# Merging eight expert matrices after a gate: a half block by TensorE, one wide chain on VectorE, and tile 5 of the last norm on GpSimd

## The chip, the cores and the metric

The kernel runs on one core of a Trainium2 chip (trn2). The metric is the device time of one execution in microseconds (us); the median of several runs is compared. Engines are called as in the profile: PE (TensorE), PEld (its weight loads), DVE (VectorE), ACT (ScalarE), POOL (GpSimd) and SP (the queue that issues the DMAs).

## The reference

One layer of a graph network on 1250 nodes of 512 features: a graph convolution (two rounds), a linear attention, and at the end a feed-forward block whose weights are merged by a gate. Only the last part is touched:

```python
gh = relu(x @ gfc1_w.T + gfc1_b)
g = (gh @ gfc2_w.T + gfc2_b).mean(over nodes)       # 8 numbers, one for each expert
W1m = W1 + sum_e g[e] * tv_W1[e]                    # 256 x 512
b1m = b1 + g @ tv_b1
W2m = W2 + sum_e g[e] * tv_W2[e]                    # 512 x 256
b2m = b2 + g @ tv_b2
h = relu(x @ W1m.T + b1m)
res = x + h @ W2m.T + b2m
out = x_before + layernorm(res) * lng + lnb
```

Here `x` is the normalised input of the block. Nothing of the merged weights can be computed before the gate is known, and the gate needs a sum over all nodes.

## The kernel before, in words

Nodes are tiled by 128 (`NT` = 10 tiles, the last of 98 rows), features by 128 (`DT` = 4 chunks), the hidden size 256 is `FT` = 2 halves. The layer runs in stages; from `last_order` on, the order of instructions on every engine is the order of the program text, so a line that stands earlier is also queued earlier on its engine, and an engine works through its own queue strictly in that order.

After the gate products (L1278, L1281) `gate` (L1297, DVE) holds the eight numbers on every partition, and `gate9` (L1298, ACT) holds them as columns. The merged first weight `m1` has four chunks `c` of 128 x 256, the merged second weight `m2` has two halves of 128 x 512. Each is a sum of nine terms. Two helpers make such sums:

- `merge` (L1309): ACT writes the first scaled term into a PSUM bank (`scaled`, L1307), DVE adds seven scaled terms one after the other (L1312), and a last addition (L1315) adds the unscaled weight. With `alone=True` DVE does all of it.
- `merge_far` (L1317): ACT scales each of the eight terms in place, POOL adds each to the weight (L1320).

Chunk 0 of `m1` is made by DVE alone, chunks 1 and 2 by `merge`, chunk 3 by ACT and POOL (L1347), the first half of `m2` by `merge` and the second by `merge_far`. `joined(c)` (L1322) multiplies chunk `c` with the transposed input into six PSUM banks, `parts`: two halves of the hidden size by three column blocks of 418, 416 and 416 nodes. After chunk 3 ACT applies the ReLU (L1328) and writes `a_t`. The vector `b2` (the merged bias) is one product (L1334), copied by ACT (L1342), and is added to the input `xn2` tile by tile: tiles 0 to 4 by DVE (L1364), 5 to 9 by POOL (L1366). PSUM has eight banks: six `parts` and two `sums`.

The last loop makes each tile `t` of the output: `out_product` (L1374, two products of 512 columns), `out_sum` (adds `xn2`), `out_gauge` (mean and variance), and then one of two endings. `out_far` normalises on ACT and does two additions or products of 512 on POOL. `out_near` does three instructions on DVE (L1413 to L1416). For the tiles in `BY_SCALAR` ACT computes the variance (L1398) instead of DVE. These lists and the delay of the near tiles stand in two places:

```python
NEAR, BY_SCALAR = (4, 5, 7, 8, 9), (5, 7, 8, 9)
for t in range(NT + 3):
    for u in NEAR:
        if u == t - (3 if u in BY_SCALAR else 1):
            out_near(u)
```

Each tile's store is issued on SP, in the order of the tiles.

Of the kernel before, what the change touches and what calls it, by code (L numbers as in the profile page):

```python
# [9 lines left out]
F32 = mybir.dt.float32  # L10
# [31 lines left out]
CHUNKS = [(0, 418), (418, 416), (834, 416)]  # L42


def rows(t):
    return min(P, N - t * P)
# [479 lines left out]
def usual_block(  # L526
# [23 lines left out]
    nc = tc.nc  # L550
# [3 lines left out]
    tmp = ctx.enter_context(tc.tile_pool(name="tmp", bufs=2))  # L554
# [7 lines left out]
    def bank(dtype=F32):  # L562
        return psum.tile([P, 512], dtype, tag="bank", name="bank")
# [14 lines left out]
    ident = const.tile([P, P], F32, name="ident")  # L578
# [49 lines left out]
    def v(name, i=0, n=1):  # L628
        at = _COLS[name][0] + i
        return v_sb[:, at:at + n]  # L630
# [43 lines left out]
    g2bc = const.tile([NE, 1], F32, name="g2bc")  # L674
# [108 lines left out]
    key = e_d  # L783
# [352 lines left out]
    gate9 = late.tile([NE + 1, P], F32, name="gate9")  # L1136
# [137 lines left out]
    pg, pg9 = bank(), bank()  # L1274
# [20 lines left out]
    gate_products([DT - 1])  # L1295
    gate = late.tile([P, NE], F32, name="gate")
    nc.vector.scalar_tensor_tensor(gate, pg[:, 0:NE], 1.0 / N, v("g2b", 0, NE), op0=ALU.mult, op1=ALU.add)  # L1297
    nc.scalar.activation(gate9[0:NE, :], pg9[0:NE, 0:P], AF.Identity, bias=g2bc, scale=1.0 / N)  # L1298

    a_t = more.tile([P, FT, N], F32, tag="E", name="a_t")
    parts = [(f, b, bank()) for f in range(FT) for b in range(len(CHUNKS))]
    sums = [bank(), bank()]

    def scaled(dst, e, src):
        nc.scalar.activation(dst, src, AF.Copy, scale=gate[:, e:e + 1])  # L1307

    def merge(acc, dst, srcs, at, alone=False):  # L1309

        for e in range(0 if alone else 1, NE):
            nc.vector.scalar_tensor_tensor(dst[at] if alone and e == NE - 1 else acc, srcs[e][at], gate[:, e:e + 1],  # L1312
                                           dst[at] if alone and e == 0 else acc, op0=ALU.mult, op1=ALU.add)
        if not alone:
            nc.vector.tensor_tensor(dst[at], acc, dst[at], ALU.add)  # L1315

    def merge_far(dst, srcs, at):  # L1317
        for e in range(NE):
            scaled(srcs[e][at], e, srcs[e][at])
            nc.gpsimd.tensor_tensor(dst[at], dst[at], srcs[e][at], ALU.add)  # L1320

    def joined(c):  # L1322
        for f, b, ps in parts:
            c0, cn = CHUNKS[b]
            nc.tensor.matmul(ps[:, :cn], m1[:, c, f * P:(f + 1) * P], xn2_t[:, c, c0:c0 + cn],
                             start=(c == 0), stop=(c == DT - 1))
# [3 lines left out]
    def first(c):  # L1330
        return (slice(None), c, slice(None))


    nc.tensor.matmul(sums[1], gate9, r9[:, 0, :], start=True, stop=True)  # L1334
    b2 = late.tile([P, D], F32, name="b2")
# [24 lines left out]
    joined(3)  # L1360
    for t in range(NT):
        n = rows(t)
        if t < NT // 2:
            nc.vector.tensor_tensor(xn2[0:n, t, :], xn2[0:n, t, :], sums[0][:n], ALU.add)  # L1364
        else:
            nc.gpsimd.tensor_tensor(xn2[0:n, t, :], xn2[0:n, t, :], b2[:n], ALU.add)  # L1366

    last = {}

    def out_product(t):  # L1370
        n = rows(t)
        last[t] = bank()
        for f in range(FT):
            nc.tensor.matmul(last[t][:n], a_t[:, f, t * P:t * P + n], m2[:, f, :], start=(f == 0), stop=(f == FT - 1))  # L1374


    NEAR, BY_SCALAR = (4, 5, 7, 8, 9), (5, 7, 8, 9)

    def out_sum(t):
        n = rows(t)  # L1380
        ps = last[t]
        if t in BY_SCALAR:
            mv = small.tile([P, 2], F32, name="mv")
            nc.vector.scalar_tensor_tensor(ps[:n], ps[:n], 1.0, xn2[0:n, t, :], op0=ALU.mult, op1=ALU.add,
                                           accum_out=mv[:n, 0:1])
            last[t] = ps, mv
        else:
            nc.vector.tensor_tensor(ps[:n], ps[:n], xn2[0:n, t, :], ALU.add)

    def out_gauge(t):  # L1390

        n = rows(t)
        if t in BY_SCALAR:
            ps, mv = last[t]
            rs = small.tile([P, 2], F32, name="rs")
            m = out_row(t)
            nc.scalar.mul(mv[:n, 0:1], mv[:n, 0:1], -1.0 / D)
            nc.scalar.activation(m[:n], ps[:n], AF.Square, bias=mv[:n, 0:1], accum_out=mv[:n, 1:2])  # L1398
            nc.scalar.activation(rs[:n, 0:1], mv[:n, 1:2], AF.Sqrt, bias=eps[:n], scale=1.0 / D)
            last[t] = ps, mv, rs, m  # L1400
        else:
            last[t] = (last[t],) + spread(last[t][:n], n) + (None,)

    def out_row(t):
        tag, bufs = (("row", 3), ("xt", 4))[t % 2]
        return tmp.tile([P, D], F32, tag=tag, bufs=bufs, name="m")

    def out_near(t):

        n = rows(t)  # L1410
        ps, mv, rs, m = last[t]
        m = out_row(t) if m is None else m
        nc.vector.scalar_tensor_tensor(ps[:n], ps[:n], mv[:n, 0:1], ln_g[:n],  # L1413
                                       op0=ALU.add if t in BY_SCALAR else ALU.subtract, op1=ALU.mult)
        nc.vector.reciprocal(rs[:n, 0:1], rs[:n, 0:1])  # L1415
        nc.vector.scalar_tensor_tensor(m[:n], ps[:n], rs[:n, 0:1], x_sb[0:n, t, :], op0=ALU.mult, op1=ALU.add)  # L1416
        nc.sync.dma_start(out=out[t * P:t * P + n, :], in_=m[:n])

    def out_far(t):

        n = rows(t)
        ps, mv, rs, _ = last[t]
# [88 lines left out]
```

## Time and profile before

| what | value |
|---|---|
| median of 3 runs | 571.74 us (571.64 to 572.16) |
| the profiled execution | 570.89 us, its span 569.1 us |
| `gate` is written | at 517.2 us of the span |
| first product with `m1` (L1325) | at 521.5 us |
| first product with `m2` (L1374) | at 540.4 us |
| last product ends | at 557.7 us |
| last instruction of DVE ends | at 563.2 us |

The span is the time from the first to the last instruction in one execution with the profiler on; the time of that execution is longer by 1.8 us, and the median of the runs without a profile lies 0.85 us above that. A row of the profile names the line, the engine, the operation, the tiles (out<-in), the shape and the count; durations are of one instruction, and on a pipelined engine the distance from one start to the next can be shorter than the duration. A product of f32 operands appears as two records on PE.

### The profile page before, as it was taken

What the parts mean: (1) busy time and instruction counts of PE and PEld (TensorE: products, weight loads), DVE (VectorE), ACT (ScalarE), POOL (GpSimd) and SP (SyncE); (2) the same over time, 40 slices, a digit from 0 to 9 for tenths busy, and PEclk for the clock granted to TensorE, in tenths of its full rate; (3) what the DMA queues carried; (4) which work ended last, traced back from release to release, by engine and by line L of the source; (5) the groups of instructions that cost most, each with busy time, mean ns of one, the idle gap of its engine ahead of it and who ended that gap; (6) DMA issues with size and microseconds to landing.
All of it is one profiled execution on the core that took longest, in us unless ns stands there. A gap on an engine that the chain in (4) does not pass through costs nothing. (4 is left out here: it accounts for less than half of the span.)

```text
span 569.1 us, 6958 instructions
## 1 busy us (share of the span) xinstructions
PE 545.6 (96%) x2367; PEld 368.1 (65%) x2367; DVE 324.7 (57%) x1097; ACT 244.2 (43%) x539; POOL 75.3 (13%) x73
## 2 busy tenths in 40 slices
PE   8799999999999999999999999999999999997992
PEld 7655568799955567777754454449995556864540
DVE  4579999976899724444425534121112248726885
ACT  6676664554354212223333344112333446726453
POOL 8200000000000000000004331000000001204972
PEclk9999999999999999999999999999999999997997
DMA  9500200020021010000311102000008320402014
GB/s 282 184 1 1 74 2 1 1 75 2 1 94 56 0 75 0 1 1 2 104 44 37 37 1 74 0 0 1 2 0 282 124 74 1 147 1 75 0 41 146
DMA packets 19285, 29.10 MB, mean 51 GB/s; under 512 B 1529, under 2 KB 8185, under 8 KB 19240
## 3 DMA queue, kind: packets, MB, share of 16 engines
q1 hardware_dynamic: 19096, 28.52, 14.8%
q8 instruction: 20, 0.33, 0.2%
q14 instruction: 25, 0.20, 0.1%
q10 hardware_dynamic: 144, 0.05, 0.0%
HBM read 26.01 MB, written 2.56 MB: 50 GB/s over the span
## 5 line engine op out<-in xcount | busy, mean ns | idle before, releaser
L981 PE MATMUL bank<-adj,y_h 128*128 128x416 f32 (+1 forms) x240 | 86.5, 361 | 1.1 <-DVE adj L851 1.1
L834 DVE TENSOR_SCALAR oh_k<-count,e_d 128x240 f16<-128x240 f16 x324 | 84.4, 281 | 0.0
L981 PE MATMUL bank<-adj,y_l 128*128 128x416 f32 (+1 forms) x240 | 84.4, 352 | 0.0
L1083 POOL TENSOR_TENSOR m<-m,ls_bc 128x512 f32<-128x512 f32 (+1 forms) x10 | 12.7, 1270 | 447.6 <-ACT m L600 447.6
L968 PE MATMUL bank<-w,h_t 128*128 128x512 f32 (+1 forms) x160 | 70.4, 592 | 0.0
L576 PE MATMUL bank<-z_t,w 128*128 128x416 f32 (+1 forms) x192 | 68.9, 513 | 0.0
L576 PEld LDWEIGHTS bank<-z_t,w 128*128 128x128 f32 x192 | 36.1, 189 | 31.8 <-issue 30.0
L832 DVE TENSOR_SCALAR oh_s<-count,s_lo 128x128 f16<-128x128 f16 x220 | 55.8, 254 | 0.0
L968 PEld LDWEIGHTS bank<-w,h_t 128*128 128x128 f32 (+1 forms) x160 | 29.4, 188 | 34.8 <-issue 34.5
L614 DVE SCALAR_TENSOR_TENSOR z_t<-u,m_sb,z_t 128x416 f32<-128x416 f32 (+1 forms) x24 | 15.7, 652 | 59.8 <-ACT u L613 59.8
L981 PEld LDWEIGHTS bank<-adj,y_h 128*128 128x128 f32 x240 | 45.1, 188 | 2.6 <-issue 2.1
L981 PEld LDWEIGHTS bank<-adj,y_l 128*128 128x128 f32 x240 | 45.2, 188 | 1.2 <-issue 0.7
L849 PE MATMUL bank<-oh_k,oh_s 128*128 128x240 f16 x324 | 41.8, 266 | 1.6 <-ACT oh_s L818 1.2
L849 PEld LDWEIGHTS <-oh_s 128*128 128x128 f16 x324 | 31.6, 98 | 16.4 <-issue 5.3
L612 ACT ACTIVATE z_t<-bank,v_sb 128x416 f32<-128x416 f32 (+1 forms) x24 | 14.7, 610 | 61.4 <-PE bank L981 61.4
L851 DVE TENSOR_TENSOR adj<-adj,bank 128x240 f32 x81 | 32.7, 404 | 13.9 <-PE bank L849 12.5
L995 DVE BATCH_NORM_STATS2 bst<-bank 128x6 f32<-128x416 f32 (+1 forms) x24 | 14.4, 600 | 42.9 <-ACT h_t L994 42.9
L917 PE MATMUL bank<-kk,xn 128*128 128x128 f32 (+1 forms) x320 | 38.4, 275 | 0.0
L576 PE MATMUL bank<-xn_t,lw 128*128 128x256 f32 (+2 forms) x128 | 36.6, 428 | 0.8 <-ACT xn_t L607 0.8
L917 PEld LDWEIGHTS bank<-kk,xn 128*128 128x128 f32 (+1 forms) x320 | 37.0, 192 | 0.1
L1064 PE MATMUL bank<-mixer,q_t 128*128 128x512 f32 (+1 forms) x80 | 36.3, 592 | 0.0
L576 PE MATMUL bank<-xn_t,gw 128*128 128x256 f32 (+2 forms) x128 | 35.3, 427 | 0.9 <-ACT xn_t L607 0.9
(172 smaller groups left out, 797.3 us busy)
## 6 DMA issues: line engine op xcount, KB each, us to landing
t<-in_tv_w SPq DMA_DIRECT2D x12, 512.0 KB, 7.6
w<-in_conv_w SPq DMA_DIRECT2D x4, 1024.0 KB, 5.4
x_in<-in_x SPq DMA_DIRECT2D x9, 256.0 KB, 4.7
xt<-in_x SPq DMA_DIRECT2D x9, 256.0 KB, 4.2
out<-m SPq DMA_DIRECT2D x9, 256.0 KB, 2.7
rest<-in_tv_w SPq DMA_DIRECT2D x4, 512.0 KB, 5.1
lw<-in_lin_w SPq DMA_DIRECT2D x4, 256.0 KB, 5.1
wk<-in_w_qkv SPq DMA_DIRECT2D x1, 1024.0 KB, 7.1
```

The lines of the kernel that those rows point to most:

```text
L576: nc.tensor.matmul(ps[:, :cn], lhs(c), rhs(c), start=(c == 0), stop=(c == k - 1))
L612: nc.scalar.activation(dst, ps[:, :cn], AF.Relu, bias=v(*bias))
L614: nc.vector.scalar_tensor_tensor(dst, u[:, :cn], minus(*slope), dst, op0=ALU.mult, op1=ALU.add)
L832: nc.vector.tensor_scalar(oh_s[:, j, :], count16[:, 0:P], s_lo[:, b, j:j + 1], None, op0=ALU.is_equal)
L834: nc.vector.tensor_scalar(oh_k[:, j, :], count16, key[:, b, j:j + 1], None, op0=ALU.is_equal)
L849: nc.tensor.matmul(ps[:, 0:NT * W], oh_s[:, j, :], oh_k[:, j, :], start=(j == 0), stop=(j == J - 1))
L851: nc.vector.tensor_tensor(adj_r[:, :, at], adj[:, :, at], ps[:, 0:NT * W].rearrange("p (s d) -> p s d", s=NT), ALU.add)
L917: nc.tensor.matmul(ps[:, c * P:(c + 1) * P], xn[0:n, t, c * P:(c + 1) * P], k_nodes(f)[0:n, t, :], start=(t == 0), stop=(t == NT - 1))
L968: nc.tensor.matmul(ps[:n], h_t[:, c, t * P:t * P + n], w1[:, c, :], start=(c == 0), stop=(c == DT - 1))
L981: nc.tensor.matmul(ps[:, :cn], y[0:n, s, f * P:(f + 1) * P], adj_r[0:n, s, c0:c0 + cn], start=(s == 0 and y is ys[0]), stop=(s == NT - 1 a ...
L995: nc.vector.bn_stats(st[:, b, :], ps[:, :cn])
L1064: nc.tensor.matmul(ps[:n], q_t[:, h, t * P:t * P + n], mixer[:, h, :], start=(h == 0), stop=(h == DT - 1))
```

## The change

- The first 128 columns of chunk 0 of `m1` are summed by PE: a product of the identity with the unscaled weight, and eight products whose stationary operand is an identity scaled by `gate[e]` (`gated`, six made by DVE, two by ACT). ACT copies the sum from PSUM to `m1`. The other 128 columns are a chain of eight on DVE, as before but half as wide.
- Chunk 1 of `m1` is made by ACT and POOL. Chunks 2 and 3 are one chain on DVE of 512 columns.
- `gate9` is scaled later, and the product for `b2` and its copy move behind `joined(1)`. `b2` is copied once; tiles 0 to 5 of `xn2` are shifted by DVE from the PSUM bank, tiles 6 to 9 by POOL.
- The second half of `m2` is begun (two of eight terms) ahead of that copy, the rest follows it.
- The order of `parts` changes: by column block first. In `joined(3)` only the first four products come ahead of the output tiles; the last two, for the third column block, come ahead of tile 5.
- Tile 5 leaves `NEAR` and `BY_SCALAR`, so POOL ends six tiles and DVE four; the delay of the `BY_SCALAR` tiles is 2 in place of 3.

```diff
-    nc.scalar.activation(gate9[0:NE, :], pg9[0:NE, 0:P], AF.Identity, bias=g2bc, scale=1.0 / N)
...
-    parts = [(f, b, bank()) for f in range(FT) for b in range(len(CHUNKS))]
+    parts = [(f, b, bank()) for b in range(len(CHUNKS)) for f in range(FT)]
...
-    nc.tensor.matmul(sums[1], gate9, r9[:, 0, :], start=True, stop=True)
-    merge(sums[0][:, 0:FF], m1, t1s, first(0), alone=True)
...
-    scaled(t1s[0][first(3)], 0, t1s[0][first(3)])
-    nc.scalar.copy(b2, sums[1])
-    scaled(sums[1][:, 0:FF], 0, t1s[0][first(1)])
+    gated = [tmp.tile([P, 2, P], F32, tag="xt", bufs=4, name="gated") for _ in range(NE // 2)]
+    one = [flat(t, 1, 2) for t in t1s]
+    two = [flat(t, 2, 4) for t in t1s]
+    for e in (0, 1, 2, 4, 5, 6):
+        nc.vector.tensor_scalar(gated[e // 2][:, e % 2, :], ident, gate[:, e:e + 1], None, op0=ALU.mult)
+    scaled(gated[1][:, 1, :], 3, ident)
+    merge_far(flat(m1, 1, 2), one, [0])
+    scaled(gated[3][:, 1, :], 7, ident)
+    merge_far(flat(m1, 1, 2), one, [1, 2])
+    nc.tensor.matmul(sums[1][:, 0:P], ident, m1[:, 0, 0:P], start=True, stop=False)
     for e in range(NE):
-        if e:
-            scaled(t1s[e][first(3)], e, t1s[e][first(3)])
-        nc.gpsimd.tensor_tensor(m1[first(3)], m1[first(3)], t1s[e][first(3)], ALU.add)
-    joined(0)
-    scaled(sums[0][:, 0:FF], 0, t1s[0][first(2)])
-    merge(sums[1][:, 0:FF], m1, t1s, first(1))
-    joined(1)
-    merge_far(m2, t2s, first(1))
-    scaled(sums[1], 0, t2s[0][first(0)])
-    merge(sums[0][:, 0:FF], m1, t1s, first(2))
-    joined(2)
+        nc.tensor.matmul(sums[1][:, 0:P], gated[e // 2][:, e % 2, :], t1s[e][:, 0, 0:P],
+                         start=False, stop=(e == NE - 1))
+    acc = sums[0][:, 0:FF - P]
+    for e in range(NE):
+        nc.vector.scalar_tensor_tensor(m1[:, 0, P:FF] if e == NE - 1 else acc, t1s[e][:, 0, P:FF], gate[:, e:e + 1],
+                                       m1[:, 0, P:FF] if e == 0 else acc, op0=ALU.mult, op1=ALU.add)
+    nc.scalar.copy(m1[:, 0, 0:P], sums[1][:, 0:P])
+    joined(0, sorted(parts, key=lambda p: p[0]))
+    merge_far(flat(m1, 1, 2), one, [3])
+    scaled(sums[1], 0, two[0])
+    merge_far(flat(m1, 1, 2), one, range(4, NE))
     nc.vector.tensor_reduce(mb1, mb, AX.X, ALU.add)
+    merge(sums[1], flat(m1, 2, 4), two)
     nc.gpsimd.tensor_tensor(mb1, mb1, v("fb1", 0, FT), ALU.add)
-    nc.scalar.copy(sums[0], b2)
-    merge(sums[1], m2, t2s, first(0))
-    joined(3)
...
+    nc.scalar.activation(gate9[0:NE, :], pg9[0:NE, 0:P], AF.Identity, bias=g2bc, scale=1.0 / N)
...
+    far2 = [t[:, 1, :] for t in t2s]
+    merge_far(m2[:, 1, :], far2, range(2))
+    joined(1, parts)
+    nc.tensor.matmul(sums[0], gate9, r9[:, 0, :], start=True, stop=True)
+    nc.scalar.copy(b2, sums[0])
+    shifted(0)
+    scaled(sums[1], 0, t2s[0][:, 0, :])
+    merge(sums[1], m2[:, 0, :], [t[:, 0, :] for t in t2s])
+    merge_far(m2[:, 1, :], far2, range(2, NE))
+    joined(2, parts)
+    joined(3, parts[0:4])
+    for t in range(1, NT):
+        shifted(t)
...
-    NEAR, BY_SCALAR = (4, 5, 7, 8, 9), (5, 7, 8, 9)
+    NEAR, BY_SCALAR = (4, 7, 8, 9), (7, 8, 9)
...
-    for t in range(NT + 3):
+    for t in range(NT + 2):
         for u in NEAR:
-            if u == t - (3 if u in BY_SCALAR else 1):
+            if u == t - (2 if u in BY_SCALAR else 1):
                 out_near(u)
+        if t == 5:
+            joined(3, parts[4:])
         if t < NT:
```

In the changed kernel the same steps have these lines: the identities L1339, their products L1344 and L1346, the narrow chain L1350, the copy of the half block L1352, `gate9` L1361, the product for `b2` L1373 and its copy L1374, the output products L1390.

More of the change, by code (lines that the diff above doesn't have):

```diff
@@ L1307, in scaled, with flat, merge, merge_far @@
         nc.scalar.activation(dst, src, AF.Copy, scale=gate[:, e:e + 1])
[L1309 to L1323, printed above, removed]
+    def flat(w, c0, c1):
+        return w[:, c0:c1, :].rearrange("p c f -> p (c f)")
+    def merge(acc, dst, srcs):
+        for e in range(1, NE):
+            nc.vector.scalar_tensor_tensor(acc, srcs[e], gate[:, e:e + 1], acc, op0=ALU.mult, op1=ALU.add)
+        nc.vector.tensor_tensor(dst, acc, dst, ALU.add)
+    def merge_far(dst, srcs, es):
+        for e in es:
+            scaled(srcs[e], e, srcs[e])
+            nc.gpsimd.tensor_tensor(dst, dst, srcs[e], ALU.add)
+    def joined(c, which):
+        for f, b, ps in which:
             c0, cn = CHUNKS[b]
@@ L1328, in joined @@
                 nc.scalar.activation(a_t[:, f, c0:c0 + cn], ps[:, :cn], AF.Relu, bias=mb1[:, f:f + 1])
-    def first(c):
-        return (slice(None), c, slice(None))
-    nc.tensor.matmul(sums[1], gate9, r9[:, 0, :], start=True, stop=True)
-    b2 = late.tile([P, D], F32, name="b2")
-    merge(sums[0][:, 0:FF], m1, t1s, first(0), alone=True)
     mb = late.tile([P, FT, NE], F32, name="mb")
@@ L1353, in usual_block @@
-    scaled(sums[1], 0, t2s[0][first(0)])
-    merge(sums[0][:, 0:FF], m1, t1s, first(2))
-    joined(2)
+    b2 = late.tile([P, D], F32, name="b2")
+    gated = [tmp.tile([P, 2, P], F32, tag="xt", bufs=4, name="gated") for _ in range(NE // 2)]
[4 more added lines that the diff above has]
+    scaled(gated[1][:, 1, :], 3, ident)
@@ L1356, in usual_block @@
+    nc.scalar.copy(m1[:, 0, 0:P], sums[1][:, 0:P])
[3 more added lines that the diff above has]
+    merge_far(flat(m1, 1, 2), one, range(4, NE))
     nc.vector.tensor_reduce(mb1, mb, AX.X, ALU.add)
+    merge(sums[1], flat(m1, 2, 4), two)
     nc.gpsimd.tensor_tensor(mb1, mb1, v("fb1", 0, FT), ALU.add)
-    nc.scalar.copy(sums[0], b2)
-    merge(sums[1], m2, t2s, first(0))
-    joined(3)
-    for t in range(NT):
+    nc.scalar.activation(gate9[0:NE, :], pg9[0:NE, 0:P], AF.Identity, bias=g2bc, scale=1.0 / N)
@@ L1362, in usual_block, with shifted @@
+    def shifted(t):
         n = rows(t)
-        if t < NT // 2:
+        if t < 6:
             nc.vector.tensor_tensor(xn2[0:n, t, :], xn2[0:n, t, :], sums[0][:n], ALU.add)
```

## The prediction

> **What bounds the kernel now.** The built program's order shows no moved instruction ahead of `gate` (L1297), so I read section 1 of the page for the whole, then for the last 55 us the table by stretches, the waits, the order of time and the clock. Times are us of the profiled execution.
>
> ```profile
> PE 545.6 (96%) x2367; PEld 368.1 (65%) x2367; DVE 324.7 (57%) x1097; ACT 244.2 (43%) x539; POOL 75.3 (13%) x73
> ```
>
> PE is the bound of the whole; the question is where it is not. The table by stretches (stretch, length, busy us of PE, PEld, DVE, ACT, POOL, granted clock, DMA share, GB/s):
>
> ```profile
> 515.00:520.00 5.00, 3.54 (x20) 1.88 (x18) 2.89 (x8) 2.35 (x6) 0.94 (x2) 0.87 0.59 211
> 520.00:525.00 5.00, 3.48 (x5) 1.85 (x6) 4.72 (x10) 5.00 (x12) 3.92 (x6) 0.50 0.01 3
> 525.00:530.00 5.00, 5.00 (x15) 2.71 (x14) 4.72 (x12) 4.33 (x8) 4.76 (x5) 0.95 0.00 0
> ...
> 560.00:565.00 5.00, 0.00 (x0) 0.00 (x0) 3.04 (x7) 0.34 (x2) 0.00 (x0) 0.81 0.72 254
> ```
>
> PE lacks work around 520 and after 557.7, and at 520 to 525 its clock is halved. The waits name the hole:
>
> ```profile
> PE bank L1325 <- DVE m L1312: 2.5, 1, 2.5
> ```
>
> The order of time (start, length, engine, line) shows what follows it, and POOL's sums beside it:
>
> ```profile
> 521.52 19.04 PE L1325 MATMUL bank<-xn_t,m 128*128 128x418 f32 x48 [2.54 <-DVE m L1312]
> ...
> 526.19 2.62 POOL L1320 TENSOR_TENSOR m<-m,t 128x512 f32<-128x512 f32 x2
> ...
> 528.89 5.32 POOL L1320 TENSOR_TENSOR m<-m,rest 128x512 f32<-128x512 f32 x4
> ...
> 534.29 2.62 POOL L1320 TENSOR_TENSOR m<-m,t 128x512 f32<-128x512 f32 x2
> ...
> 540.40 17.33 PE L1374 MATMUL bank<-m,a_t 128*128 128x512 f32 x40
> ```
>
> From 521.52 PE never waits: 24 products of 418 or 416 columns (two records each), then 20 of 512. POOL's half of m2 is whole at 536.9, 3.5 us before PE wants it. Last the clock:
>
> ```profile
> 518.60:518.70 0.10, 0.10 (x1) 0.97 1.05 410
> 518.70:518.80 0.10, 0.10 (x1) 0.50 0.95 372
> 525.40:525.50 0.10, 0.10 (x1) 0.50 0.00 0
> 525.50:525.60 0.10, 0.10 (x1) 0.90 0.00 0
> 563.00:563.10 0.10, 0.00 (x0) 0.83 0.85 328
> ```
>
> It falls at 518.69, returns at 525.51, and falls again at 563.03. From 521.52 PE runs 4.0 us at half speed: 2.0 us lost.
>
> **Units, from the rows.** PE: 0.70 per 418-column product (records 0.35 apart), 0.867 per 512-column one (17.33/20), 0.24 per 128-column one (two records; L917 288 records in 34.9), drain 0.17. DVE, start to start: 0.524 for a 256-wide chain step, 0.79 for 512, so 0.39 for 128 by the same slope; final TENSOR_TENSOR 0.69. ACT: 0.40 and 0.62 start to start for 256 and 512 (lasting 0.50, 0.71). POOL: 0.80 and 1.35 for dependent sums of 256 and 512, 1.23 for independent ones. A handover is 0.03 to 0.08.
>
> **The change, part by part.**
>
> *Identities.* L1334 (K=9) leaves the hole; nine 128-column products enter it. No row has a 128-wide f32 TENSOR_SCALAR: the lower bound is the 0.17 from start to start of the 128-wide f16 row (L832), the upper the 0.33 of a 324-wide f32 one (L785); I take 0.20, since 128 f32 elements lie close to the former. Six take 1.2, ACT's two run beside them, so PE's chain is bound by itself: 517.6 + 8 x 0.24 = 519.5. ACT copies the half block (0.39 by slope; done 520.1) and PE starts at 520.13: 1.39 earlier. DVE's eight 128-wide steps end at 517.25 + 1.2 + 3.1 = 521.6, before PE has done three products (522.2): hidden.
>
> *Second chunk, now POOL's.* POOL starts at 518.1 and its eight 256-wide sums, 0.80 apart, end at 524.7; before, the same sums began at 518.2, waited 1.75 for ACT, and were wanted only for the last chunk. PE is through its six products at 520.13 + 4.2 = 524.33: it waits 0.4. ACT's copy of the half block stands among these scalings and costs POOL nothing while POOL is behind. The last product of chunk 0 takes the bank that the moved `gate9` scaling (L1361) reads; that is done at 523.0, the product is due at 523.6: hidden.
>
> *Wide chain.* Seven 512-wide steps and the sum end at about 527.9; PE asks for chunks 2 and 3 only after chunk 1 (528.95) and the moved b2 product L1373 (0.87, now on PE's path): 529.8. Hidden by 1.9.
>
> *The moved b2 copy is what costs.* In ACT's order `nc.scalar.copy(b2, sums[0])` follows the first two far scalings and waits for L1373 (529.98 with drain). ACT has been free since about 524.4; queued behind the copy are DVE's start of m2 and the six remaining far scalings, so POOL, idle since 527.6, waits too. Copy to 530.6, start value for DVE 531.34, first scaling done at 531.96; POOL 532.02 + 5 x 1.35 + 1.27 = 540.04, against 536.9 before. DVE: shift of tile 0 (0.6), 7 x 0.79 + 0.69 from 531.4: 537.6. PE has done chunk 2 and four products of chunk 3 at 529.81 + 7.0 = 536.81. It waits 0.86 for DVE's half of m2, does one product, and waits 1.55 for POOL's.
>
> *Last products.* From 540.09: 19 x 0.867 + two moved products 1.40 = 17.87. Their two ReLUs stand on ACT behind tile 3's norm and tile 4's Sqrt (until 550.2) and end at 551.4, while PE asks for tile 6 at 551.0: wait 0.45. PE ends at 558.4; before 557.6 (without drain): **+0.8**. The ledger: start -1.39, clock -2.0, b2 product +0.87, waits 0.41 + 0.86 + 1.55 + 0.45 = +3.27; sum +0.75.
>
> *End.* Before, DVE did three endings of 1.55 each after tile 9's sum. Now two are left, since the delay is 2 and tile 5 goes to POOL, but tile 9's sum comes 0.6 late behind tile 7's ending: 4.4 from PE's end to DVE's, before 5.3: **-0.9**. POOL: four shifts end at 545.0, six tiles of 2.58 end at 560.6, 2.3 before DVE ends near 563.0. SP's ten stores keep their number; one more waits for POOL, one fewer for DVE, and the store queued behind tile 6's (560.6) is tile 7's, 1.3 us later than its data and not the last.
>
> Sum: +0.8 - 0.9 = -0.1 on an end of 563.17; the 5.9 us from there to the span's end and the 1.8 around the span (570.89 in all) stay. The median of the runs shown, 571.74, is 0.85 above this execution; I take the difference over.
>
> **Two rules against it.** *Port.* The first chain step (t1 and m1 both in SBUF) took 0.549 where the others took 0.489, while POOL's small `mb` sum ran: 0.06. The Trainium skill, SBUF — State Buffer, "Who interferes with whom", says that a VectorE instruction in a 2-port mode (tensor_scalar among them), or with two SBUF inputs, and a GpSimd instruction that reads SBUF exclude each other for a whole instruction. Then the fifth and sixth identity and the first 128-wide step can each stand behind a POOL sum of 0.725. Worked through, PE's chain ends 0.17 later and DVE's up to 1.3 later (522.9), which costs 0.7 at most at chunk 0, mostly covered by the 0.4 wait behind it: +0.15 to +0.25. By the row +0.06. I take +0.1.
>
> *Clock.* The row: 518.69, 525.51 and 563.03 lie 2 and 11 times 3.41 apart, so the clock is judged over stretches of 3.41, and 515.28 to 518.69 was judged idle though PE showed work in it: records of 8 moving columns, 8 weight columns or 9 rows. The stretch 556.2 to 559.6 held 1.5 us of full products (44%) and brought no fall. TensorE: Matmul & The Clock Gate, "What's actually happening", has the same free-running window and asks for a whole idle one. After the change the stretch to 518.69 holds 1.1 us of full 128x128 products (32%). By the rule no fall: -2.0, as in the ledger. By the row, where a stretch with something in it fell, 32% is undecided. I take no fall, since dense products are nearer to the 44% case, and keep the fall as a rival.
>
> Forecast: 571.74 - 0.1 + 0.1 = about 571.7.
>
> **The rivals.**
>
> *1. The clock still falls (slower).* Place: 518.69, in the identity chain. The last four identities run at 0.48, PE starts at 520.95. If the stretch to 522.10 (83% busy) counts as busy, the loss reaches the end as +1.0: 572.7. At the kernel's start the stretch from 0.2 to 3.6 held 2.0 us of transposes (60%) and brought no full speed (22 took 4.95, 0.22 each, to 6.5, where four took 0.50 at 497.6), so 83% is open. If not, PE is at half speed to 525.51, chunk 0 ends at 527.4 instead of 524.3, and b2's copy, POOL and everything after shift by 2.7: 574.4. It decides once chunk 0 ends after POOL's chunk 1 at 524.7. Chances 0.14 and 0.23.
>
> *2. More gain than counted (faster).* The stretches of 3.41 do not start with the kernel, so other executions return to full speed between about 524 and 527.5, and before loses 1.3 to 3.0. The 0.85 by which the runs exceed the profiled one speaks for more than 2.0, their narrow range (0.52) against a wide spread. If the change ends a loss of 3.0, it gives 570.6; with POOL's six sums at 1.23 instead of 1.35 (against: they depend on each other) 570.0. Chance 0.13.
>
> *3. ACT's order doesn't hold POOL.* If the copy came early, POOL would end m2 before 537 and 1.5 more would be gained; the built order has the copy behind both scalings and its wait on PE, so I give it nothing of its own.
>
> **How the numbers follow.** A measurement of this kernel can tell about 0.2% (1.14 us) from no change: 570.6 to 572.9. The forecast keeps 0.50, with +-0.8 for slopes and waits (570.9 to 572.5 mostly): 0.04 faster, 0.40 same, 0.06 slower. Rival 1: 0.07 same, 0.30 slower. Rival 2: 0.13 faster. Together faster 0.17, same 0.47, slower 0.36. The range 570.4 to 574.2 leaves out the upper half of the 574.4 case (0.12) and the best of rival 2 (0.07).
>
> **What would show it.** Right: L1325 begins near 520.1 with a full clock; a wait of ACT's copy on L1373 of about 5 us; POOL idle 4 us before its third far sum; PE waits of 0.9 and 1.5 before L1390; DVE ends 4.4 after PE. Wrong: 0.50 in the clock around 520 to 525, identities standing behind L1320 on DVE, or m2 whole before 538.

## The result, and the profile after

The changed kernel takes 572.16 us (median of 12 runs, 571.60 to 573.44), the kernel before 571.69 (12 runs beside them, 570.53 to 572.45): the ratio is 1.0011, 95% interval [1.0003, 1.002]. The forecast was 571.7, no change. The time lies in the range given, and the change is a loss of about 0.5, less than the 0.2% named as what a measurement can tell, but not nothing. The profiled execution took 572.21, its span 570.3. Its `gate` (L1297) starts at 517.90 in place of 517.05, so rows after it are compared by their distance from that start.

Section 1 of the page of the changed kernel (busy us, share of the span, instructions):

```profile
PE 548.1 (96%) x2385; PEld 370.6 (65%) x2385; DVE 324.0 (57%) x1095; ACT 243.4 (43%) x540; POOL 76.8 (13%) x74
```

Its table by stretches (stretch, length, busy us of PE, PEld, DVE, ACT, POOL, granted clock, DMA share, GB/s):

```profile
515.00:520.00 5.00, 5.00 (x36) 3.86 (x34) 2.22 (x9) 2.48 (x7) 1.10 (x3) 1.00 0.53 185
520.00:525.00 5.00, 4.64 (x17) 2.68 (x16) 4.68 (x12) 4.35 (x11) 4.39 (x6) 1.00 0.08 30
525.00:530.00 5.00, 4.64 (x14) 2.20 (x12) 3.95 (x6) 0.06 (x1) 3.37 (x5) 1.00 0.00 0
...
540.00:545.00 5.00, 3.63 (x10) 1.66 (x10) 4.04 (x9) 0.39 (x2) 4.92 (x5) 1.00 0.02 3
```

The hole around 520 is filled and the clock never falls there. In its place there is a new one: at 525 to 530 ACT works for 0.06 us of 5, and at 540 to 545 PE lacks work. The waits from 517 on (who waits, for whom; total, times, longest) name the cause in the same order:

```profile
ACT b L1374 <- PE bank L1373: 6.4, 1, 6.4
POOL m L1320 <- ACT rest L1306: 4.8, 1, 4.8
DVE xn L1366 <- ACT b L1374: 2.9, 1, 2.9
...
PE bank L1390 <- POOL m L1320: 1.4, 1, 1.4
...
DVE bank L1429 <- ACT m L1414: 0.5, 1, 0.5
```

The order of time on PE (start, length, engine, line, tiles, shape, records; in brackets the idle time before):

```profile
518.50 2.17 PE L1346 MATMUL bank<-t,gated 128*128 128x128 f32 x16
521.03 4.47 PE L1325 MATMUL bank<-xn_t,m 128*128 128x418 f32 x12 [0.36 <-ACT m L1352]
525.86 4.46 PE L1325 MATMUL bank<-xn_t,m 128*128 128x418 f32 x12 [0.35 <-POOL m L1320]
530.25 1.12 PE L1373 MATMUL bank<-r,gate 9*128 9x512 f32 x2
531.30 7.27 PE L1325 MATMUL bank<-xn_t,m 128*128 128x418 f32 x20
538.96 1.10 PE L1390 MATMUL bank<-m,a_t 128*128 128x512 f32 x2 [0.39 <-ACT a_t L1328]
541.43 7.99 PE L1390 MATMUL bank<-m,a_t 128*128 128x512 f32 x18 [1.37 <-POOL m L1320]
549.26 1.56 PE L1325 MATMUL bank<-xn_t,m 128*128 128x416 f32 x4
550.65 8.75 PE L1390 MATMUL bank<-m,a_t 128*128 128x512 f32 x20
```

Beside the wait at 538.96 stand the last step of DVE's half of `m2` and ACT's four ReLUs. DVE's half ends at 538.86, 0.10 ahead of the product. Of the ReLUs the third ends at 538.52 and the last at 539.22, behind the product's start. So the wait is for DVE's half, although the row of PE names ACT.

```profile
538.17 0.69 DVE L1315 TENSOR_TENSOR m<-bank,m 128x512 f32<-128x512 f32 x1
...
536.57 2.65 ACT L1328 ACTIVATE a_t<-bank,mb 128x418 f32<-128x418 f32 x4 [0.28 <-PE bank L1325]
```

The sums of the second half of `m2` on POOL: two ahead of ACT's wait, six behind it.

```profile
525.91 2.62 POOL L1320 TENSOR_TENSOR m<-m,t 128x512 f32<-128x512 f32 x2
533.36 5.32 POOL L1320 TENSOR_TENSOR m<-m,rest 128x512 f32<-128x512 f32 x4 [4.83 <-ACT rest L1306]
538.75 2.62 POOL L1320 TENSOR_TENSOR m<-m,t 128x512 f32<-128x512 f32 x2
```

PE ends at 559.40, 41.50 after `gate`'s start (before 40.68): +0.82. Last the end, DVE's rows first and then two of ACT's:

```profile
559.05 0.76 DVE L1429 SCALAR_TENSOR_TENSOR bank<-bank,mv,ln_g 128x512 f32<-128x512 f32 x1 [0.49 <-ACT m L1414]
...
560.57 0.69 DVE L1400 SCALAR_TENSOR_TENSOR bank<-bank,xn 98x512 f32<-98x512 f32 x1
...
557.33 0.78 ACT L600 ACTIVATE m<-bank,rs 128x512 f32<-128x512 f32 x1
...
558.23 0.69 ACT L1414 ACTIVATE m<-bank,mv 128x512 f32<-128x512 f32 x1
```

At 559.05 DVE's ending of tile 7 has waited 0.49 for the variance of tile 7, which stands on ACT behind the norm of tile 6 (L600). Tile 9's sum (560.57) stands on DVE behind that ending. DVE ends at 564.35, 4.95 after PE; before, 5.44 after PE.

### The profile page after: what moved, and what is told of

It reads as the page before. It is cut to its first block, busy times and chain, and to the rows that moved or that the text cites. A ratio compares the mean times of both kernels' runs of the same rounds, so it can differ in the third digit from the quotient of the medians.

```text
span 570.3 us, 7008 instructions
## 1 busy us (share of the span) xinstructions
PE 548.1 (96%) x2385; PEld 370.6 (65%) x2385; DVE 324.0 (57%) x1095; ACT 243.4 (43%) x540; POOL 76.8 (13%) x74
## 3 DMA queue, kind: packets, MB, share of 16 engines
HBM read 26.01 MB, written 2.56 MB: 50 GB/s over the span
## 5 line engine op out<-in xcount | busy, mean ns | idle before, releaser
L834 DVE TENSOR_SCALAR oh_k<-count,e_d 128x240 f16<-128x240 f16 x324 | 83.1, 276 | 0.0
```

The lines of the kernel that those rows point to most:

```text
L834: nc.vector.tensor_scalar(oh_k[:, j, :], count16, key[:, b, j:j + 1], None, op0=ALU.is_equal)
```

## The experiments

Every kernel below was profiled and timed beside the kernel before. Distances are from the start of `gate` in its profiled execution; that of kernel 5 holds a stretch at half clock, told there.

| kernel | PE ends | DVE ends | DVE behind PE | ratio to before, 95% interval |
|---|---|---|---|---|
| before | 40.68 | 46.12 | 5.44 | 1 |
| changed | 41.50 | 46.45 | 4.95 | 1.0011 [1.0003, 1.002] |
| 1 late copy of `b2` | 39.24 | 44.18 | 4.94 | 0.997 [0.9958, 0.9981] |
| 2 before, PE kept busy | 39.26 | 44.71 | 5.45 | 0.9976 [0.9969, 0.9983] |
| 3 before, new lists | 40.70 | 46.72 | 6.02 | 1.0023 [1.0015, 1.003] |
| 4 no identities | 44.06 | 49.00 | 4.94 | 1.0044 [1.0029, 1.0059] |
| 5 old lists | 43.21 | 48.65 | 5.44 | 1.0019 [1.0012, 1.0025] |
| 6 ScalarE's order | 41.61 | 46.55 | 4.94 | 1.0016 [1.001, 1.0023] |
| 7 late copy, early product | 38.61 | 43.55 | 4.94 | 0.9967 [0.9955, 0.9979] |
| 8 as 2, `mb1` early | 38.71 | 44.16 | 5.45 | 0.9973 [0.9967, 0.998] |
| 9 swap at tile 7 | 41.49 | 45.80 | 4.31 | 1.0015 [1.0008, 1.0022] |
| 10 as 7, with the swap | 38.61 | 42.92 | 4.31 | 0.9963 [0.995, 0.9976] |
| 11 filler in PE's wait | 41.49 | 46.44 | 4.95 | 1.0016 [1.0009, 1.0022] |
| 12 no products set aside | 40.11 | 46.13 | 6.02 | 1.0006 [0.9998, 1.0015] |

**1. The copy of `b2` behind all far scalings** (on the changed kernel)

```diff
-    merge_far(m2[:, 1, :], far2, range(2))
+    merge_far(m2[:, 1, :], far2, range(NE))
     joined(1, parts)
     nc.tensor.matmul(sums[0], gate9, r9[:, 0, :], start=True, stop=True)
-    nc.scalar.copy(b2, sums[0])
-    shifted(0)
     scaled(sums[1], 0, t2s[0][:, 0, :])
     merge(sums[1], m2[:, 0, :], [t[:, 0, :] for t in t2s])
-    merge_far(m2[:, 1, :], far2, range(2, NE))
+    nc.scalar.copy(b2, sums[0])
...
-    for t in range(1, NT):
+    for t in range(NT):
         shifted(t)
```

> The changed kernel with one order altered: ScalarE scales all eight far terms of the second half of m2 first, then writes VectorE's start value, and only then copies b2; tile 0 is shifted after VectorE's chain. Theory A (ScalarE's queue behind the b2 copy holds GpSimd and VectorE, and TensorE's wait of 1.4 us before its second product with m2 is that): GpSimd has m2 whole near 536.8 of the changed kernel's own positions, 4.5 us earlier than its 541.4; the 1.4 us wait is gone; the end moves by -1.6 us against the changed kernel, to about 570.5 with before at 571.7 (ratio 0.998). Theory B (TensorE's start and the clock set the end, the wait is taken up elsewhere): no move against the changed kernel, ratio 1.001.

The order of time on PE:

```profile
530.80 7.27 PE L1325 MATMUL bank<-xn_t,m 128*128 128x418 f32 x20
537.91 8.75 PE L1388 MATMUL bank<-m,a_t 128*128 128x512 f32 x20
```

Both waits ahead of the products with `m2` are gone, and PE ends 2.26 earlier after the gate (41.50 to 39.24). The ratio is 0.997 in place of 1.0011: one copy that stood too early on ACT (with tile 0's shift, which needs it and moves along) cost more than the whole change lost.

**2. PE kept busy in the hole** (on the kernel before)

```diff
+    def keep_warm():
+        for _ in range(8):
+            nc.tensor.transpose(parts[5][2][:, 0:P], ident, ident)
+
+    keep_warm()
     nc.tensor.matmul(sums[1], gate9, r9[:, 0, :], start=True, stop=True)
+    keep_warm()
```

> The kernel before with 16 extra transposes of the identity in the hole of TensorE before chunk 0 (8 on each side of the b2 product), into a bank that the first products overwrite; nothing else changes. Theory A (the hole makes the clock fall, and that costs the kernel before 2.0 us): no half clock around 519 to 525 and an end 2.0 us earlier, about 569.7 (ratio 0.9965). Theory B (transposes do not count as activity, or the clock falls in another stretch as well): clock as before, ratio 1.000 or a little above.

The order of time on PE:

```profile
521.61 17.07 PE L1325 MATMUL bank<-xn_t,m 128*128 128x418 f32 x48 [1.10 <-DVE m L1312]
...
539.85 16.55 PE L1380 MATMUL bank<-m,a_t 128*128 128x512 f32 x38 [0.31 <-ACT a_t L1328]
```

The 24 products take 17.07 in place of 19.04: the granted clock is 1.00 at 518 to 526, and that is worth 1.97, with nothing else of the change. Some of it is given back (PE ends 1.42 earlier): its waits show a ReLU 7.4 behind POOL's addition to `mb1`, which stands behind the eight far sums.

```profile
ACT a_t L1328 <- POOL mb L1363: 7.4, 1, 7.4
```

**3. Only the new lists of the last norm** (on the kernel before)

```diff
-    NEAR, BY_SCALAR = (4, 5, 7, 8, 9), (5, 7, 8, 9)
+    NEAR, BY_SCALAR = (4, 7, 8, 9), (7, 8, 9)
...
-    for t in range(NT + 3):
+    for t in range(NT + 2):
...
-            if u == t - (3 if u in BY_SCALAR else 1):
+            if u == t - (2 if u in BY_SCALAR else 1):
```

> The kernel before with the last loop of the changed one alone: tile 5 ended by ScalarE and GpSimd, delay 2 in place of 3. Theory A (my prediction's -0.9 for the end): VectorE ends 4.4 us after TensorE's last product instead of 5.4, ratio 0.9985. Theory B (as the changed kernel's trace has it, ScalarE's variance of tile 7 comes late and VectorE waits 0.5 for it, 4.9 us from TensorE's end): -0.5 us, ratio 0.999. Theory C (GpSimd with six tiles ends last): GpSimd's last sum after 561.5, no gain, ratio 1.000.

The order of time on DVE:

```profile
559.06 0.76 DVE L1413 SCALAR_TENSOR_TENSOR bank<-bank,mv,ln_g 128x512 f32<-128x512 f32 x1 [1.50 <-ACT m L1398]
```

Slower, where every theory said faster or equal. PE ends as before (40.70 against 40.68), DVE 0.60 later: its ending of tile 7 waits 1.50 for ACT's variance, queued behind the norms of tiles 5 and 6. That stands against the step *End* of the prediction.

**4. No identities** (on the changed kernel): chunk 0 by DVE's chain of eight, 256 wide

```diff
-    gated = [tmp.tile([P, 2, P], F32, tag="xt", bufs=4, name="gated") for _ in range(NE // 2)]
...
+    nc.scalar.activation(gate9[0:NE, :], pg9[0:NE, 0:P], AF.Identity, bias=g2bc, scale=1.0 / N)
+    merge_far(flat(m1, 1, 2), one, [0, 1, 2])
+    acc = sums[0][:, 0:FF]
     for e in range(NE):
-        nc.vector.scalar_tensor_tensor(m1[:, 0, P:FF] if e == NE - 1 else acc, t1s[e][:, 0, P:FF], gate[:, e:e + 1],
-                                       m1[:, 0, P:FF] if e == 0 else acc, op0=ALU.mult, op1=ALU.add)
-    nc.scalar.copy(m1[:, 0, 0:P], sums[1][:, 0:P])
+        nc.vector.scalar_tensor_tensor(m1[:, 0, :] if e == NE - 1 else acc, t1s[e][:, 0, :], gate[:, e:e + 1],
+                                       m1[:, 0, :] if e == 0 else acc, op0=ALU.mult, op1=ALU.add)
```

> The changed kernel without the identities: chunk 0 is one chain of eight 256-wide steps on VectorE as before, and gate9 is scaled first on ScalarE (0.27 us); everything else as in the changed kernel. Theory A (the identities are worth an earlier start of 1.4 us and the full clock, worth 2.0): the clock falls at about 0.6 us after the last of the small gate products' stretch and is half for 4 us of chunk 0, chunk 0 ends 3 us later, the b2 product and all behind it shift: +2.9 us against the changed kernel, about 575 (ratio 1.006). Theory B (TensorE has slack to its later waits): below +1.5 us, ratio under 1.0035.

The order of time on PE:

```profile
521.47 10.45 PE L1325 MATMUL bank<-xn_t,m 128*128 128x418 f32 x24 [4.24 <-ACT t L1306]
```

The table by stretches of the same kernel (the clock is the number after POOL's):

```profile
519.00:520.00 1.00, 0.00 (x0) 0.00 (x0) 0.93 (x3) 1.00 (x3) 0.92 (x2) 0.50 0.37 143
```

PE starts 4.52 after the gate in place of 3.13, and the clock is halved again: PE ends 2.56 later than in the changed kernel. Theory A, nearly to the number: the identities do what the prediction gave them, an earlier start and a clock that holds. In time the loss is smaller, 1.7 (573.83 against 572.16), between the two theories' numbers; in the profiled executions the difference lies ahead of the gate, which starts 0.95 earlier here.

**5. The old lists of the last norm** (on the changed kernel)

```diff
-    NEAR, BY_SCALAR = (4, 7, 8, 9), (7, 8, 9)
+    NEAR, BY_SCALAR = (4, 5, 7, 8, 9), (5, 7, 8, 9)
...
-    for t in range(NT + 2):
+    for t in range(NT + 3):
...
-            if u == t - (2 if u in BY_SCALAR else 1):
+            if u == t - (3 if u in BY_SCALAR else 1):
```

> The changed kernel with the old last norm: tile 5 in NEAR and BY_SCALAR again, five tiles ended by VectorE, delay 3. It undoes the tail alone. Theory A (the prediction's step: the new tail shortens the end by 0.9): 0.9 slower than the changed kernel, ratio to before about 1.0027. Theory B (the end is always about 5.44 after PE's last product with the old tail, 4.95 with the new one): 0.5 slower, about 1.002. Theory C (the run with only the new lists on the kernel before, 1.0023: the new lists cost time, because from tile 5 on the norms on VectorE and ScalarE set the end and ScalarE's variance of tile 7 stands behind two norms): 0.6 to 1.2 faster than the changed kernel, ratio 0.999 to 1.000, and no wait of over 1 us of a VectorE ending for that variance.

The ratio, 1.0019, is theory B's number, and so is the distance from PE's end to DVE's (5.44); its interval overlaps that of the changed kernel, and the medians (572.22 and 572.16) hardly differ. So no gain of the new lists is shown in time here, and on the kernel before (run 3) they lose 0.6: a gain of 0.9 is seen in neither. The profile held something else. PE ends 1.71 later than in the changed kernel, all of it here, in the order of time on PE:

```profile
540.53 9.69 PE L1390 MATMUL bank<-m,a_t 128*128 128x512 f32 x18 [1.37 <-POOL m L1320]
```

The same eighteen records take 7.99 in the changed kernel. Its table by stretches shows the clock (the number after POOL's):

```profile
540.40:540.50 0.10, 0.00 (x0) 0.00 (x0) 0.10 (x1) 0.00 (x0) 0.10 (x2) 1.00 0.00 0
540.50:540.60 0.10, 0.07 (x1) 0.07 (x1) 0.10 (x1) 0.00 (x0) 0.10 (x1) 0.93 0.00 0
540.60:540.70 0.10, 0.10 (x1) 0.10 (x2) 0.10 (x1) 0.00 (x0) 0.10 (x1) 0.50 0.00 0
...
543.90:544.00 0.10, 0.10 (x1) 0.00 (x0) 0.10 (x1) 0.00 (x0) 0.10 (x1) 0.51 0.00 0
544.00:544.10 0.10, 0.10 (x2) 0.06 (x1) 0.07 (x2) 0.00 (x0) 0.10 (x2) 1.00 0.00 0
```

It fell at 540.6, when PE's wait for POOL had just ended, and came back 3.4 later. The changed kernel has the same wait. So the change closed one gap in PE's work and opened another that can do the same, in some executions.

**6. ScalarE's order at the start** (on the changed kernel)

```diff
     scaled(gated[1][:, 1, :], 3, ident)
-    merge_far(flat(m1, 1, 2), one, [0])
     scaled(gated[3][:, 1, :], 7, ident)
-    merge_far(flat(m1, 1, 2), one, [1, 2])
+    merge_far(flat(m1, 1, 2), one, [0, 1, 2])
```

> The changed kernel with ScalarE's order at the start changed: both gated identities first, then the three scalings for chunk 1, so that GpSimd's first sum starts about 0.35 later and VectorE's identities run more of their time without it. Theory A (a VectorE TENSOR_SCALAR and a GpSimd sum hold each other off): the six identities take 1.2 to 1.5 in place of 1.80 and the first product with m1 starts 0.2 to 0.5 earlier after the gate; GpSimd's chunk 1 ends about 0.3 later, so the end moves by no more than 0.2 (ratio to before 1.000 to 1.0015). Theory B (an identity costs 0.30 to 0.37 alone): still 1.8, the start unchanged.

The six identities in the order of time on DVE, first the changed kernel, then this one:

```profile
518.11 1.80 DVE L1339 TENSOR_SCALAR gated<-ident,gate 128x128 f32<-128x128 f32 x6
```

```profile
517.63 1.32 DVE L1339 TENSOR_SCALAR gated<-ident,gate 128x128 f32<-128x128 f32 x6
```

Starting POOL's first sum 0.29 later takes 0.48 off DVE's six. All of it is in the sixth, here by itself in the changed kernel:

```profile
519.15 0.76 DVE L1339 TENSOR_SCALAR gated<-ident,gate 128x128 f32<-128x128 f32 x1
```

It starts 0.11 behind POOL's first sum (at 519.04, 0.78 long) and ends 0.09 behind that sum's end; in this run the sixth takes 0.28. Theory A holds for DVE, but PE's start moves by only 0.13 (less than the 0.2 to 0.5 expected), and PE then waits 0.57 for POOL's chunk 1 in place of 0.35. The time is the same.

**7. The product for `b2` in PE's first wait** (on kernel 1)

```diff
-    joined(1, parts)
     nc.tensor.matmul(sums[0], gate9, r9[:, 0, :], start=True, stop=True)
+    joined(1, parts)
```

> The kernel with the late copy of b2 (all eight far scalings ahead of it), and in addition the product for b2 ahead of the six products of chunk 1, where PE waits 0.36 for GpSimd. Theory A (the product on PE's path costs 0.87 less the part that a wait covers): the wait goes, 0.35 faster than the late copy alone, ratio to before about 0.9963 where that had 0.997. Theory B (gate9 is not ready there, or the rest of the path has slack): no gain, 0.997.

By the trace PE ends 0.63 earlier than in kernel 1: the product now lies where PE would have waited for POOL. The times (569.26 and 569.62) agree in sign; 0.9967 and 0.997 can't be told apart.

**8. `mb1` early** (on kernel 2)

```diff
     merge(sums[1][:, 0:FF], m1, t1s, first(1))
...
+    nc.vector.tensor_reduce(mb1, mb, AX.X, ALU.add)
...
+    nc.gpsimd.tensor_tensor(mb1, mb1, v("fb1", 0, FT), ALU.add)
     merge_far(m2, t2s, first(1))
...
-    nc.vector.tensor_reduce(mb1, mb, AX.X, ALU.add)
-    nc.gpsimd.tensor_tensor(mb1, mb1, v("fb1", 0, FT), ALU.add)
```

> The kernel before with sixteen identity transposes that keep the clock up, and in addition mb1 made earlier (its reduction after the chain of chunk 0, GpSimd's addition ahead of the eight far sums of m2), so that the ReLUs don't stand behind these sums. Theory A (of the 2.0 that the clock is worth, 0.6 were given back because the ReLUs waited for mb1): PE's wait of 0.31 before the products with m2 goes, ratio to before 0.9963 to 0.9967 where the transposes alone had 0.9976. Theory B (the end is bound elsewhere): 0.9976.

The order of time on PE:

```profile
538.60 17.33 PE L1380 MATMUL bank<-m,a_t 128*128 128x512 f32 x40
```

No wait is left ahead of the last products; PE ends 1.97 earlier than before, the whole worth of the clock, and 0.55 earlier than in kernel 2. The ratios show little of that (0.9973 lies inside the interval of 0.9976), the medians do: 570.27 in kernel 2, 569.57 here.

**9 and 10. Tile 7's variance ahead of tile 6's norm**, on the changed kernel and on kernel 7

```diff
+        if t == 7:
+            out_gauge(t)
         if 0 < t <= NT and t - 1 not in NEAR:
             out_far(t - 1)
-        if t < NT:
+        if t < NT and t != 7:
             out_gauge(t)
```

> The changed kernel with ScalarE's variance of tile 7 queued ahead of the norm of tile 6. Theory A (the new tail is held by that variance, which stands behind two norms; VectorE's ending of tile 7 waits 0.49 for it and tile 9's sum stands behind that ending): the wait goes and VectorE ends about 4.4 after PE's last product in place of 4.95; GpSimd has tile 5 until then, so tile 6 loses nothing; 0.5 faster than the changed kernel, ratio to before about 1.0005. Theory B (the end is set elsewhere): 4.9 as before, ratio 1.0011 to 1.0016.

> The kernel with the late copy of b2 and its product ahead of chunk 1, with the same swap of tile 7's variance and tile 6's norm. Theory A: 0.5 faster than without the swap, ratio to before about 0.9957 where that had 0.9967. Theory B: 0.9967.

Kernel 9, the order of time on DVE:

```profile
557.90 0.76 DVE L1429 SCALAR_TENSOR_TENSOR bank<-bank,mv,ln_g 128x512 f32<-128x512 f32 x1
...
559.42 0.69 DVE L1400 SCALAR_TENSOR_TENSOR bank<-bank,xn 98x512 f32<-98x512 f32 x1
```

The wait is gone, and DVE ends 4.31 after PE in both kernels, where 4.94 or 4.95 stood: that was the queue on ACT. In time it is nearly nothing: 1.0015 in place of 1.0011, and 0.9963 in place of 0.9967. By the traces half of the 0.6 is given back behind DVE's end, where the last stores stand: from `gate` to the end of the span the changed kernel takes 52.40, kernel 9 52.10. SP issues the last three stores within 1.57 in kernel 9 and 2.40 in the changed one. That these stores, closer together, are what gives it back was not tried by itself. Kernel 10 has the lowest ratio of all; its interval overlaps those of kernels 1, 2, 7 and 8.

**11. A filler in PE's wait** (on the changed kernel)

```diff
             nc.tensor.matmul(last[t][:n], a_t[:, f, t * P:t * P + n], m2[:, f, :], start=(f == 0), stop=(f == FT - 1))
+            if t == 0 and f == 0:
+                for _ in range(8):
+                    nc.tensor.transpose(parts[3][2][:, 0:P], ident, ident)
```

> The changed kernel with eight identity transposes (about 1.05 us, into a bank that is free) between the two products of output tile 0, where PE waits 1.4 for GpSimd's half of m2. Theory A (the wait is long enough to let the clock fall in about one execution of six, as it did at 540.6 in the profiled execution of the changed kernel with the old tail, 3.4 us at half speed, 1.7 lost): none of some twenty executions lies more than 1 above the median, where 4 of 21 and 4 of 22 did; the median stays, ratio 1.001 to 1.0015. Theory B (the slow executions have another cause): still about one in six.

The order of time on PE:

```profile
540.12 1.04 PE L1393 MATMUL bank<-ident 128*128 128x128 f32 x8
541.65 7.99 PE L1390 MATMUL bank<-m,a_t 128*128 128x512 f32 x18 [0.50 <-POOL m L1320]
```

None of its 22 executions lies more than 1 above their median (571.64 to 573.11). Without the filler, with the same wait, these did: 1 of 12 of the changed kernel, 1 of 5 of kernel 4, 4 of 21 of kernel 5, 2 of 22 of kernel 6 (two more, which the expectation counted, by only 0.8 or 0.9), 4 of 22 of kernel 9, together 12 of 82. Were the filler idle, none in 22 would come about in some 3 cases of 100 (70/82 to the power of 22). In eleven of the twelve the mean granted clock of the execution (0.986 to 0.989) is below that of every other execution of the same kernel. So theory A is likely. But a clock that falls in this wait is not the only source of such executions: kernel 8, which has no such wait, has 4 of 22 more than 1 above its median, at clocks (0.989 to 0.991) that its fastest ones have too. The median stays as expected: 572.37.

**12. No products set aside** (on the changed kernel)

```diff
-    joined(3, parts[0:4])
+    joined(3, parts)
...
-        if t == 5:
-            joined(3, parts[4:])
```

> The changed kernel with all six products of the last chunk ahead of the output tiles, as before the change: the last two are no longer set aside for tile 5. Theory A (these two, 1.40 on PE, would fill the wait of 1.37 for GpSimd's half of m2, which setting them aside left empty): the wait shrinks to about 0.4 or goes, PE ends 1.2 to 1.4 earlier, ratio to before 0.9985 to 0.999, and no execution with a second fall of the clock. Theory B (the ReLUs become late instead, or the tail is bound by VectorE): less than 0.5 faster, ratio over 1.000.

The order of time, a row of PE and one of DVE:

```profile
541.35 16.58 PE L1390 MATMUL bank<-m,a_t 128*128 128x512 f32 x38 [0.62 <-POOL m L1320]
...
558.65 0.76 DVE L1429 SCALAR_TENSOR_TENSOR bank<-bank,mv,ln_g 128x512 f32<-128x512 f32 x1 [1.50 <-ACT m L1414]
```

PE ends 1.39 earlier, as theory A had it: setting the two products aside left the wait empty. But DVE ends only 0.32 earlier, because its ending of tile 7 now waits 1.50 for ACT, exactly as in run 3. Theory B is right on the time: under 0.5 (1.0006). One of its 13 executions still lies 1.1 above the median; its mean clock, 0.989, is also that of an execution below the median, so whether it fell in the wait stays open. At the end PE was no longer the bound.

## Why the prediction was right and wrong

In short: up to the sum of output tile 0 on DVE (24.69 after the gate, before 25.26) the change gains 0.57, though the early copy of `b2` takes 2.26 of it away (run 1). From that sum to DVE's end (21.76, before 20.86) it loses 0.90, where the step *End* had a gain of 0.9. Together that is +0.33. The rows, before and changed, first and last of the stage:

```profile
542.31 0.70 DVE L1388 TENSOR_TENSOR bank<-bank,xn 128x512 f32<-128x512 f32 x1 [3.63 <-PE bank L1374]
...
562.42 0.75 DVE L1416 SCALAR_TENSOR_TENSOR m<-bank,rs,x_sb 98x512 f32<-98x512 f32 x1
```

```profile
542.59 0.70 DVE L1404 TENSOR_TENSOR bank<-bank,xn 128x512 f32<-128x512 f32 x1 [0.75 <-PE bank L1390]
...
563.60 0.75 DVE L1432 SCALAR_TENSOR_TENSOR m<-bank,rs,x_sb 98x512 f32<-98x512 f32 x1
```

The prediction counted by PE's end instead. The ledger up to PE's end, from the rows of the changed kernel shown above (products at 0.70 and 0.867 as in the prediction):

| step | predicted | measured | from |
|---|---|---|---|
| start of PE | -1.39 | -1.34 | 3.13 after `gate`'s start, before 4.47 |
| clock | -2.0 | -1.97 | 19.04 to 17.07 in run 2 |
| product for `b2` | +0.87 | +1.24 | 525.86 + 6 x 0.70 to 531.30 |
| chunk 1 by POOL | +0.41 | +0.63 | 521.03 + 6 x 0.70 to 525.86 |
| first product with `m2` | +0.86 | +0.66 | 531.30 + 10 x 0.70 to 538.96 |
| POOL's half of `m2` | +1.55 | +1.60 | 538.96 + 0.867 to 541.43 |
| tile 6 for the ReLUs | +0.45 | 0 | no wait there |
| PE's end | +0.75 | +0.82 | 41.50, before 40.68 |
| *End* | -0.9 | -0.49 | 4.95, before 5.44 |
| sum, without the port | -0.15 | +0.33 | 46.45, before 46.12 |

**Right.** The hole, the clock and what replaced them. PE starts 3.13 after the gate where 3.08 was worked out; the clock holds; the copy of `b2` waits 6.4 (about 5 was said) and POOL 4.8 for what is queued behind it; PE ends 0.82 later. The sentence that the moved copy is what costs is borne out by run 1: without it PE ends 2.26 earlier and the kernel beats the one before. PE waits for DVE's half of `m2`, as said: in run 1, where that half ends before PE needs it, the wait is gone. Rival 3 (the copy doesn't hold POOL) is out. Rival 1 was not seen: in none of the nine profiled executions with the identities does the clock fall between the gate and 540.

**Wrong: the step *End*.** It took -0.9 for one ending of 1.55 fewer on DVE, less 0.6 for tile 9's sum. DVE's own work was counted rightly: run 9 shows 4.31 from PE's end to DVE's, 4.4 was said. Left out was ACT's queue. With tile 5 given to POOL, ACT normalises tiles 5 and 6 just ahead of tile 7's variance, DVE's ending of tile 7 waits for it, and tile 9's sum stands behind. That returns 0.64 (4.95 against 4.31); less 0.09 (4.31, not 4.4) and 0.14 (before 5.44, not 5.3) it makes the 0.41 by which the step was mis-sized, nearly all of the way from -0.15 to +0.33. The deeper error is what the step took for granted, that the end hangs on PE's. From the start of tile 0's sum to DVE's end it takes

| order of the last stage | kernels | us |
|---|---|---|
| old lists | before, 2, 8 | 20.86 |
| new lists | 3, 12 | 21.44, 21.43 |
| new lists, two products set aside | changed, 1, 4, 6, 7, 11 | 21.69 to 21.76 |
| the same with the swap | 9, 10 | 21.12 |

There DVE and ACT set most of the pace: in run 12 PE was 1.39 earlier and the end followed by 0.32. The new lists cost 0.58 and the two products set aside 0.32 more. The swap takes 0.64 of the 0.90 back; what the other 0.26 is was not tried. Old lists with the products set aside (run 5) were profiled only with a stretch at half clock, so that case stays open.

**Mis-sized, smaller.** The product for `b2` costs 1.24, not 0.87: 1.05 from its start to the next product's, and 0.19 of handover ahead of it. Chunk 1 is waited for 0.22 longer than said: POOL's first three sums, the first of them beside DVE's last identity, take 2.52 in place of 2.4, and 0.30 passes ahead of the fourth. The prediction's own sum was off there too: eight sums at 0.80 from 518.1 end at 524.5, not 524.7. The ReLUs don't hold tile 6. These errors nearly cancel.

**The two rules.** *Port*: six identities, 1.80 beside POOL's sums and 1.32 with POOL's first sum 0.29 later (run 6). The rule of the Trainium skill (SBUF — State Buffer, "Who interferes with whom"), that such a pair excludes each other, named the right pair: DVE lost 0.48, in the one identity that started under a sum of POOL, far more than the row's 0.06. On PE's start it was worth 0.13, between the two figures weighed, and nothing in time. *Clock*: no fall in the identity chain, as the rule (TensorE: Matmul & The Clock Gate, "What's actually happening") would have it. Its whole idle stretch doesn't hold elsewhere: in run 5 the stretch of 3.41 that ended with the fall at 540.6 held 1.65 of PE's records, and on the kernel before the stretch up to 518.69 held 2.96.

**The time.** Of the 0.47 between the medians (572.16 and 571.69), +0.33 lies behind the gate in the two profiled executions. The rest can't be assigned: the profiled execution of before is 0.80 faster than its median, that of the changed kernel is at its median and had lost 0.85 ahead of the gate. Rival 2 has something for it: the time of the kernel before goes with its mean granted clock. Of the 51 executions beside runs 9 to 12 the 19 at 0.983 or 0.984 have a median of 572.12, the 9 at 0.991 or 0.992 one of 570.74. How much of this was lost in the hole was not recorded, and the spread of the times doesn't tell: kernel 2, with the hole filled, spreads over 1.6 too (18 executions).

## What to carry to other kernels

Before an instruction that waits for a late engine is put into a queue, list what stands behind it and who starves: here one copy on ACT idled POOL for 4.8 and DVE for 2.9, and moving it behind the work of others turned a loss of 0.1% into a gain of 0.3%. At the end of a kernel, follow every engine's queue for the last tiles, not only the engine that has too much: taking a tile from DVE put two norms of ACT ahead of the variance that DVE waits for. Count such a stage from where it begins: by the distance from PE's end the new lists seemed to gain 0.5, by the distance from tile 0's sum they lost. And a gap of PE that is closed is worth less if the change opens another; work set aside for later should be what fills it.

## What the runs showed of the hardware

- The clock also fell after a gap in PE's work of only 1.4. In run 5 the stretch 537.18 to 540.59 held 1.65 of PE's records (48%), and the clock was halved from 540.6 to 544.0. In the kernel before, a stretch with 1.5 (44%) in it brought no fall, and the one up to the fall at 518.69 held 2.96 (87%), nearly all of it products with 8 columns or 9 rows. So a busy share of the records doesn't decide it alone; what does stays open. With that gap 12 of 82 executions took over 1 more than the median.
- Sixteen products of the identity with itself, issued as transposes, were enough, with the product for `b2` between them, to hold the clock at 1.00 through the hole (run 2).
- One identity on DVE that started under a sum of POOL took 0.76 in place of 0.28 (run 6).
- In the changed kernel's profiled execution the first tile of the input reached DVE at 3.92 in place of 3.50, although its load was issued at the same time (0.74 and 0.73), and the clock was at 0.50 from 26 to 28 where before it was full. From 29 on the lag is the 0.85 ahead of the gate. No instruction was moved there, and by the other profiles it doesn't go with the change: kernels 4 and 5, made from the changed kernel, have 3.50 and a gate at 516.95 and 516.99, and kernel 3, made from the kernel before, has 3.91 and a gate at 517.64.
